# A decoder layer's kernel: the head norm's root argument on other engines, a bank kept free, the latent in another tile, and a rewritten end

## Chip, core and metric

The kernel runs on one core of one Trainium2 chip. The metric is the device time of one execution in microseconds (us); of several runs the median is given. The engines' short names are PE (TensorE, with PEld for its weight loads), DVE (VectorE), ACT (ScalarE), POOL (GpSimd) and SP (SyncE, which here only issues transfers). A `q` behind a name is the engine's instruction queue.

## The reference

Everything is float32; 4 sequences (`b`) of 512 tokens, 512 channels. Three blocks follow each other, each with a residual sum and a layer norm (mean and variance over the channels, epsilon 1e-5):

```python
x = layernorm(x + attn(x))            # differential attention
x = layernorm(x + mamba(ctx, z=x))    # convolution, selective scan, gate
x = layernorm(x + experts(x))         # shared expert + 16 routed experts

# attn: 8 heads, each of two softmax maps; 4 groups g of two heads share k and v
p   = softmax(q1 @ k1.T * s, causal) - lam * softmax(q2 @ k2.T * s, causal)
o   = p @ v                                                # [512 tokens, 256] per head
o   = o * rsqrt(mean(o*o, -1) + 1e-5) * subln_w * (1 - LAMBDA_INIT)   # the head norm
out = concat(o) @ out_w.T + out_b

# mamba: for 512 channels d and 16 states n, along the tokens
state = state * exp(dt * A) + dt * u * B;   y = sum_n(state * C) + D * u;   y * silu(z)

# experts: xl = x @ Wdown.T (the latent, 128 wide); 8 of 16 experts by sigmoid gate
shared = (x @ sw1.T * relu(x @ swg.T)**2) @ sw2.T
acc    = sum_e w[:, e] * ((xl @ rw1[e].T * relu(xl @ rwg[e].T)**2) @ rw2[e].T)
out    = shared + acc @ Wup.T
```

## The kernel before, in words

**Recording and ordering.** The body does not issue instructions directly. `nc` is a `Notes` object that records every operation as a `Step` with the tiles it reads and writes, its engine, and a sort key: `nc.key` (a due time that the code sets for each piece of work) plus an entry of the table `SHIFT`, looked up by the output's name and the engine's first letter (`"ps_y.t"` is a matmul into `ps_y`, `.v` VectorE, `.s` ScalarE or SyncE, `.g` GpSimd). `Notes.order` then runs through the steps with a table of durations (`cost`), gives each idle engine the ready step with the lowest key, and keeps tile buffers and PSUM banks within their counts. The result is one fixed instruction order for each engine; an engine runs its own queue strictly in that order. All instructions are issued from one line, L360 (L358 for pairs of small matmuls), so the profile is read by tile names rather than lines.

**Attention.** 16 units (group `g` outside, sequence `b` inside), two heads (`hh`) each. `project_T` makes `kT` and `qT`, matmuls into `ps_v` make the values `v`, which DVE adds a bias to. For each of four query tiles `i`, `softmax` makes scores `s` and probabilities `e` with row sums `l1`, `l2`. The first map is left undivided by its row sum `l1` (the head norm takes the factor out again), so the norm's epsilon is multiplied with `l1` squared. `values` transposes `e` into `pt`, copies it to `pT`, multiplies with `v` into `po`, copies that to `o`, and squares it on ScalarE with the sum in `ms` (`sq`). After the fourth tile, DVE forms `rs = EPS * l1 * l1` and `ms = ms/256 + rs`, GpSimd raises `ms` to the power -1/2 (`rs`), ScalarE scales the four tiles of `o` by `rs`, TensorE transposes them (`pt_o`), ScalarE evicts them as `oT`, and the output projection `ps_out` is added to `res`. `pt`, `pt_o` and the other transposes share one PSUM bank.

**Scan.** For each sequence 16 states by two channel halves: DVE multiplies (`h<-du,bc`), scans (`TENSOR_TENSOR_SCAN`), multiplies again (`h<-h,bc`), and GpSimd issues the transfer that adds `h` into the DRAM tensor `y` (`y<-h`). These run all along attention and the first experts, beside TensorE's work.

**Experts.** For each sequence: gate the scan's output, transpose, norm, gate matmuls `ps_gate` (16 router columns and the latent). ScalarE copies the latent by tokens to `xr`, TensorE transposes it into `xl`. The shared expert makes `sh`. For 16 experts by two halves `k`: `pg` and `ph` matmuls, `glu` (ScalarE: relu, square; DVE: `ht`), and a matmul into `pa`, which gathers all 32 parts. `pa` of the first sequence lies in the general pool `mm` (three PSUM banks, shared with `ph`, `ps_out`, `ps_qk`, `ps_y` and others), later ones in the bank that `po` leaves. At the end `pa` is copied to `aT`, and four output tiles `ps_y` sum `aT @ w_u` and two products of `sh` with `w_s2`. DVE adds each to `res`; the last sequence's tiles are normed and stored one by one by `layernorm` (DVE: statistics, aggregate, epsilon; GpSimd: power; DVE: `nb = -mean*rs`; ScalarE: scale and shift).

**Start.** Eight matmuls of the identity (`warm`) run while the first inputs are loaded. Then come `ps_in` (the scan's input projection) and the first unit's `ps_qk`. GpSimd adds the output bias (`obb`) to the four `res` tiles early on, 4.5 us each.

Of the kernel before, what the change touches and what calls it, by code (L numbers as in the profile page):

```python
# [13 lines left out]
AF = mybir.ActivationFunctionType  # L14
# [6 lines left out]
ENGINES = ("tensor", "vector", "scalar", "gpsimd", "sync")  # L21

SHIFT = {
    "aT.s": 19.9, "a_neg.s": 36.7, "a_neg.v": -21.7, "bc.s": 12.7, "bq.s": -11, "bvb.s": 13.2, "cT.s": -0.7,
    "cb.s": -0.3, "cf.v": 2.5, "cw.s": -33.1, "da.g": -5.7, "da.s": -3.1, "db.s": 9.1, "dsk.s": -4, "dt.s": -3.6,
    "dt.v": 19.7, "du.s": 2.1, "du.v": 45.5, "e.s": 10.2, "e.v": -5.1, "gb.s": 3.8, "h.v": -4.8, "ht.v": -0.6,
    "kT.s": 17.3, "l.v": 4.6, "ln_mv.v": 1.1, "ln_nb.v": -14, "ln_rs.g": 3.8, "ln_st.v": 13, "ln_ve.v": -5.5,
    "lo.v": 6.9, "lp.v": 40.1, "ls.s": 2.8, "ls.v": -10.5, "lt.s": 3.2, "m.v": 10.9, "ms.v": -5.6, "nlam.v": -5.1,
    "o.s": -40.2, "oT.s": 3.2, "obb.s": 21.3, "ow.s": 7.5, "pT.s": 3.5, "pa.t": 1.2, "pg.t": 2.7, "pg_s.t": -3.5,
    "ph.t": 2.9, "ph_s.t": 8.6, "po.t": -3.4, "pr.s": -22.7, "pr.v": -34.8, "ps_dt.t": -22.1, "ps_gate.t": -14.1,  # L30
    "ps_in.t": -19, "ps_out.t": 5.2, "ps_qk.t": 1.6, "ps_v.t": 7.7, "ps_x.t": -7, "ps_y.t": 10.3, "pt_l.t": -7.1,
    "pt_o.t": 3.5, "pt_w.t": 2.9, "pt_x.t": -4.1, "pt_y.t": -4.7, "qT.s": 2.2, "relu.s": 2.4, "relu_s.s": -25.5,
    "res.g": -40.7, "res.s": 16, "res.v": -6.4, "rp.v": -25.4, "rs.g": 0.6, "rs.v": -5.3, "s.t": 0.9, "sc.v": 9.1,
    "sg.s": -0.9, "sg.v": 2.6, "sgc.s": 1.1, "sh.v": 6, "sp.v": 12.9, "sq.s": 7.2, "sub.s": -33, "sub.v": -20.3,
    "v.v": -7.9, "w.s": -14.5, "wT.s": -0.7, "w_dg.s": -3.6, "w_dt.s": 61.7, "w_e.s": 28.1, "w_in.s": -28,
    "w_s.s": -13.3, "w_u.s": 11, "w_xp.s": 5.5, "warm.t": 30.4, "wb.s": 2.9, "wk.s": -12.1, "wq.s": 7.5, "wv.s":
    7.6, "x2T.s": 1.4, "xT.s": 1.8, "xd.s": 27.7, "xl.s": 1.6, "xm.g": 17.6, "xm.s": 2.9, "xr.s": -4.7, "xw.v":
    6.5, "y.g": -9.3, "y.s": 6.5, "y.v": -44.5, "yb.s": 7.2, "yb.v": 0.4,
}
B, S, HID = 4, 512, 512  # L40
NT = S // P
# [7 lines left out]
C2 = 6  # L49
# [109 lines left out]
def cost(engine, name, out, ins, kw):  # L159

    n = columns(out) if isinstance(out, View) else 0
    psum = any(isinstance(v, View) and v.buf.pool.psum for v in ins)
    if engine == "tensor":
        if name == "pair":
            return 0.15 + n * 0.00168, 0.35, 0.0
        if name == "transpose":
            return 0.11 * max(1, n / 128), 0.35, 0.0
        return max(n * 0.00168, 0.13), 0.35, 0.0
    if name == "dma_start":
        size = max(v.shape[0] * columns(v) * 4 if isinstance(v, View) else 0 for v in (out, *ins))  # L170
        add = kw.get("accum_op") is not None
        return {"sync": 0.45, "gpsimd": 0.95, "scalar": 0.1}[engine], 4.2 if add else 2.3, size / 230e3 * (1 + add)
    if engine == "gpsimd":
        if any(v is ALU.pow for v in ins):
            return 1.3, 0.5, 0.0
        return 0.15 + 0.0026 * n, 0.5, 0.0
    if engine == "scalar":
        wide = isinstance(kw.get("scale"), View) or isinstance(kw.get("bias"), View)
        return (
            0.19 + 0.00079 * n + (0.1 if wide else 0.0) + (0.15 if kw.get("accum_out") is not None else 0.0), 0.3, 0.0  # L180
        )
    if name == "tensor_tensor_scan":
        return 0.05 + 0.00223 * n, 0.25, 0.0
    if name in ("tensor_reduce", "bn_stats"):
        n = columns(ins[0])
    if n <= 8:
        return 0.2, 0.25, 0.0
    if name == "scalar_tensor_tensor":
        return 0.12 + 0.00125 * n, 0.25, 0.0
    if name == "tensor_scalar" and not psum:  # L190
        return 0.1 + (0.00085 if any(isinstance(v, View) for v in ins[1:]) else 0.00058) * n, 0.25, 0.0
    return 0.13 + (0.00108 if psum else 0.0011) * n + (0.1 if name == "tensor_tensor_reduce" else 0.0), 0.25, 0.0


class Notes:
# [54 lines left out]
    def order(self, keys, window=100.0):  # L250
# [24 lines left out]
        while events:  # L275
# [11 lines left out]
            for e in ENGINES:  # L287
# [4 lines left out]
                for s in ready[e]:  # L292
                    if ready_at[s.at] > now or keys[s.at] > most:
                        continue
                    if s.name == "dma_start" and landed[e][-8] > now:
                        continue

                    if s.shares and port > now:
                        continue
                    rank = (keys[s.at] + (10.0 if s.table not in (None, table) else 0.0), s.at)  # L300
                    if best is not None and rank >= least:
                        continue

                    if all(
                        b in live
                        or free[b.pool, b.tag] >= (2 if s.name == "pair" and b.pool.psum else 1)
                        and (b.pool.psum or b in due[b.pool, b.counts[-1]][: free[b.pool, b.counts[-1]]])
                        for b in s.bufs
                    ):
                        best, least = s, rank  # L310
# [63 lines left out]
def decoder_kernel(  # L374
# [33 lines left out]
    def small(shape, tag, bufs=8):  # L408
        return sb.tile(shape, tag, tag, bufs)
# [120 lines left out]

    nc.key = -60.0
    pw = ps.tile([P, S], "tr", "warm", 1)
    for i in range(8):
        nc.tensor.matmul(pw[:, :P], lhsT=ident, rhs=ident, start=True, stop=True)


# [33 lines left out]
    def values(e, v, i, o, ms):  # L570
        w = (i + 1) * P
        pt = ps.tile([P, S], "tr", "pt", 1)
        for j in range(i + 1):
            nc.tensor.transpose(pt[:, j * P : (j + 1) * P], e[:, 0, j * P : (j + 1) * P], ident)
        pT = sb.tile([P, S], "pT", "pT", 2)
        nc.scalar.copy(pT[:, :w], pt[:, :w])
        po = ps.tile([P, 256], "po", "po", 1)
        for j in range(i + 1):
            nc.tensor.matmul(po, lhsT=pT[:, j * P : (j + 1) * P], rhs=v[:, j, :], start=(j == 0), stop=(j == i))
        nc.scalar.copy(o[:, i, :], po)  # L580
        sq = sb.tile([P, 256], "sq", "sq", 1)
        nc.scalar.activation(sq, po, AF.Square, accum_out=ms[:, i : i + 1])

    def attention(n):

# [25 lines left out]
        for hh in range(2):  # L611
# [12 lines left out]
                values(e, v, i, o, ms)  # L624

            rs = small([P, NT], "rs", 4)
            nc.vector.scalar_tensor_tensor(rs, l1, EPS, l1, ALU.mult, ALU.mult)
            nc.vector.scalar_tensor_tensor(ms, ms, 1.0 / 256, rs, ALU.mult, ALU.add)
            nc.gpsimd.tensor_tensor(rs, ms, mhalf, ALU.pow)
            for i in range(NT):  # L630
                nc.scalar.activation(o[:, i, :], o[:, i, :], AF.Copy, scale=rs[:, i : i + 1])
# [126 lines left out]
    nc.sync.dma_start(out=w_s[:, 0, :, :], in_=swgT.rearrange("(c p) n -> p c n", p=P))  # L758
    nc.sync.dma_start(out=w_s[:, 1, :, :], in_=sw1T.rearrange("(c p) n -> p c n", p=P))
    w_s2 = load([P, 2, HID], sw2T.rearrange("(c p) n -> p c n", p=P), "wq", "w_s2", 2)  # L760
    w_u = load([P, HID], wuT, "wq", "w_u", 2)

    def glu(pg, ph, dst, r):
        nc.scalar.activation(r, pg, AF.Relu)
# [3 lines left out]
    def experts(b):  # L768
# [26 lines left out]


        nc.key += 10.0
        pls, xr = [], sb.tile([P, NT, LAT], "c2", "xr", C2, 1)
        for k in range(2):
            pl = ps.tile([P, 2, 256], "mm", "ps_gate", 3)  # L800
            for i in range(2):
# [57 lines left out]
        for e in range(NE):  # L859
# [10 lines left out]
            for k in range(2):  # L870
                nc.key = t_expert(b, e + 0.5 * k)
                pg = ps.tile([P, S], "s", "pg", 3)
                nc.tensor.matmul(pg, lhsT=w_e[:, 0, k * P : (k + 1) * P], rhs=xl, start=True, stop=True)
                ph = ps.tile([P, S], "mm", "ph", 3)
                nc.tensor.matmul(ph, lhsT=w_e[:, 1, k * P : (k + 1) * P], rhs=xw, start=True, stop=True)
                ht = sb.tile([P, S], "c2", "ht", C2, 2)
                glu(pg, ph, ht, sb.tile([P, S], "e", "relu", 3, 2))
                nc.key += DOWN
                nc.tensor.matmul(
                    pa, lhsT=w_e[:, 2, k * LAT : (k + 1) * LAT], rhs=ht,  # L880
                    start=(e == 0 and k == 0), stop=(e == NE - 1 and k == 1),
                )
# [1 line left out]
        aT = sb.tile([P, S], "pT", "aT", 2)  # L884
        nc.scalar.copy(aT, pa)
        for i in range(NT):
            po = ps.tile([P, HID], "mm", "ps_y", 3)
            nc.tensor.matmul(po, lhsT=aT[:, i * P : (i + 1) * P], rhs=w_u, start=True, stop=False)
            for k in range(2):
                nc.tensor.matmul(  # L890
                    po, lhsT=sh[:, k, i * P : (i + 1) * P], rhs=w_s2[:, k, :], start=False, stop=(k == 1)
                )
            nc.vector.tensor_tensor(res[b][:, i, :], res[b][:, i, :], po, ALU.add)
            if b == B - 1:
                layernorm(res[b], res[b], (i,))
                nc.sync.dma_start(out=out[b, i * P : (i + 1) * P, :], in_=res[b][:, i, :])
        if b < B - 1:
            layernorm(res[b], res[b])
# [68 lines left out]
```

## Time and profile before

| | |
|---|---|
| median of 5 runs | 1527.24 us (1526.95 to 1529.09) |
| the profiled execution | 1526.95 us, its span 1525.2 us |
| instructions | 15976 |
| granted TensorE clock | 1.00 |
| busy: PE, DVE, ACT, POOL | 99%, 78%, 63%, 13% |

The span runs from the first to the last instruction of the program. A fp32 matmul stands in the profile as two records (two passes); with 512 columns each shows some 0.593 us, but the next one starts 0.429 us later, as they are pipelined: a PE that starts a record every 0.429 us is at its pace, and "busy" covers a little of what comes after. A wait is named by what ended it. In the busy table by stretches, each engine has its busy time and, in brackets, its number of instructions; in a chain, each row is start, duration and what ran.

### The profile page before, as it was taken

The numbers are of one execution on the slowest core, as the hardware profiler recorded it, in microseconds if no ns is written. First come the engines' busy times: TensorE is split into PE (matmuls) and PEld (weight loads), VectorE is DVE, ScalarE is ACT, GpSimd is POOL, SyncE is SP. The second block draws the span as 40 slices with busy tenths as digits, with TensorE's granted clock in tenths as the row PEclk, the third lists the DMA queues.
The fourth block names the chain that finished last, engine by engine and source line by source line (L and its number), as shares of the span: only waits on it lengthen the run. The fifth ranks groups of instructions, "written<-read, shape, count | busy, mean of one in ns | idle before, by whom it ended". The sixth has DMA issues, their size and how long they took to land.

```text
span 1525.2 us, 15976 instructions
## 1 busy us (share of the span) xinstructions
PE 1512.4 (99%) x5008; PEld 845.9 (55%) x5008; DVE 1196.3 (78%) x2036; ACT 956.6 (63%) x2130; POOL 203.6 (13%) x208
## 2 busy tenths in 40 slices
PE   9999999999999999999999999999999999999997
PEld 5566565555656656565665656655445444445443
DVE  5479899798998989998898998999889953543433
ACT  3785666668666566876556678677866553444443
POOL 4111111110211110122111111111111100000000
PEclk9999999999999999999999999999999999999999
DMA  8136686554668764466864565556866842442341
GB/s 272 57 88 107 138 188 132 98 112 97 106 132 187 131 143 71 107 131 130 180 127 113 106 116 138 126 128 133 202 156 156 220 125 70 152 126 68 109 130 39
DMA packets 105749, 196.23 MB, mean 129 GB/s; under 512 B 10977, under 2 KB 46049, under 8 KB 105665
## 3 DMA queue, kind: packets, MB, share of 16 engines
q1 hardware_dynamic: 86944, 127.57, 29.8%
q0 software_dynamic: 18432, 67.12, 25.9%
q8 instruction: 40, 0.66, 0.2%
q10 hardware_dynamic: 288, 0.52, 0.1%
q14 instruction: 45, 0.36, 0.1%
HBM read 119.28 MB, written 75.89 MB: 128 GB/s over the span
## 4 chain that ended last, share of the span: by engine, by line
PE 97%; DVE 2%; ACT 1%; issue 0%; POOL 0%; POOLq 0%; DVEq 0%
PE ps_qk L360 21%; PE ps_out L360 14%; PE s L360 9%; PE po L360 9%; PE ph L360 7%; PE ps_v L360 7%; PE pa L360 7%; PE pg L360 7%; PE ps_y L360 3%; PE pt L360 2%; PE pt_o L360 2%; PE ph_s L360 2%; PE pg_s L360 2%; PE ps_in L360 2%; PE ps_gate L360 1%; PE ps_dt L358 1%
## 5 line engine op out<-in xcount | busy, mean ns | idle before, releaser
L360 DVE TENSOR_TENSOR_SCAN h<-da,h 128x1024 f32<-128x1024 f32 x128 | 292.9, 2288 | 3.1
L360 PE MATMUL ps_qk<-xT,wq 128*128 128x512 f32 x512 | 240.8, 594 | 0.0
L360 PE MATMUL ps_out<-ow,oT 128*128 128x512 f32 x512 | 236.2, 593 | 0.0
L360 POOL DMA_DIRECT2D y<-h x128 | 111.1, 868 | 788.9 <-DVE h L360 657.4
L360 ACT ACTIVATE da<-dt,a_neg 128x512 f32<-128x512 f32 (+1 forms) x256 | 175.1, 716 | 36.1 <-DVE h L360 35.9
L360 DVE TENSOR_TENSOR ht<-relu,ph 128x512 f32<-128x512 f32 x128 | 87.6, 685 | 132.9 <-ACT relu L360 103.3
L360 ACT ACTIVATE relu<-pg 128x512 f32<-128x512 f32 x128 | 76.0, 593 | 152.9 <-PE pg L360 124.5
L360 PE MATMUL s<-kT,qT 128*128 128x384 f32 (+3 forms) x512 | 164.0, 435 | 0.0
L360 ACT ACTIVATE e<-e,nm 128x256 f32<-128x256 f32 (+3 forms) x256 | 141.6, 556 | 32.3 <-DVE nm L360 31.6
L360 PE MATMUL po<-v,pT 128*128 128x256 f32 x640 | 159.4, 380 | 0.4 <-ACT pT L360 0.4
L360 DVE CUSTOM_DVE_ANT_0 e<-s,mask 128x256 f32<-128x256 f32 (+3 forms) x256 | 119.8, 487 | 49.0 <-PE s L360 42.3
L360 DVE TENSOR_TENSOR h<-h,bc 128x1024 f32<-128x1024 f32 x128 | 156.3, 1221 | 1.2
L360 DVE TENSOR_TENSOR h<-du,bc 128x1024 f32<-128x1024 f32 x128 | 156.0, 1219 | 0.1
L360 PEld LDWEIGHTS po<-v,pT 128*128 128x128 f32 x640 | 121.4, 190 | 60.5 <-issue 37.4
L360 PEld LDWEIGHTS ps_out<-ow,oT 128*128 128x128 f32 x512 | 93.4, 191 | 87.6 <-issue 82.8
L360 PEld LDWEIGHTS ps_qk<-xT,wq 128*128 128x128 f32 x512 | 92.7, 191 | 77.3 <-issue 70.9
L360 PE MATMUL pa<-ht,w_e 128*128 128x512 f32 x256 | 131.0, 594 | 0.6 <-DVE ht L360 0.6
L360 PE MATMUL ph<-xw,w_e 128*128 128x512 f32 x256 | 130.5, 593 | 0.2 <-DVE xw L360 0.2
L360 PE MATMUL pg<-xl,w_e 128*128 128x512 f32 x256 | 129.5, 593 | 0.0
L360 PE MATMUL ps_qk<-xT,wk 128*128 128x512 f32 x256 | 121.0, 594 | 0.0
L360 PE MATMUL ps_v<-wv,xT 128*128 128x256 f32 x512 | 119.0, 380 | 1.3 <-DVE v L360 1.3
L360 PEld LDWEIGHTS s<-kT,qT 128*128 128x128 f32 x512 | 87.6, 191 | 55.2 <-issue 44.0
(123 smaller groups left out, 2006.0 us busy)
## 6 DMA issues: line engine op xcount, KB each, us to landing
y<-h POOLq DMA_DIRECT2D x128, 512.0 KB, 7.9
bc<-bc SPq DMA_DIRECT2D x64, 512.0 KB, 6.4
wb<-w SPq DMA_DIRECT2D x64, 256.0 KB, 3.6
xT<-in_xT_dram SPq DMA_DIRECT2D x15, 1024.0 KB, 7.6
w_e<-in_rwgT_dram SPq DMA_DIRECT2D x64, 128.0 KB, 2.2
w_e<-in_rw1T_dram SPq DMA_DIRECT2D x64, 128.0 KB, 2.3
w_e<-in_rw2T_dram SPq DMA_DIRECT2D x64, 128.0 KB, 2.5
wq<-in_wqkvT_dram SPq DMA_DIRECT2D x8, 512.0 KB, 8.1
```

Of the source, the lines that this page charges most:

```text
L358: self.nc.tensor.matmul(out, lhsT=lhsT, rhs=rhs, **{"start": True, "stop": True, **s.kw})
L360: getattr(getattr(self.nc, s.engine), s.name)(*[get(a) for a in s.args], **{k: get(v) for k, v in s.kw.items()})
```

## The change

- The head norm: the sum of squares is scaled by 1/256 at its source (scale 1/16 inside ScalarE's square), `rs = EPS * l1 * l1` becomes a square on ScalarE, and the sum `ms + rs` an addition on GpSimd, ahead of the power there. Both DVE instructions go.
- Banks: `ph` of the first sequence gets a name of its own with at most 2 of the 3 `mm` banks, `ps_y` at most 2. The planner's condition for taking a bank now looks at all counts of a tile.
- The latent by tokens `xr` lies in the second half of a tile whose first half is `w_u`, no longer in a buffer of the pool `c2`.
- The ends: 5 warm-up matmuls for 8; each `ps_y` sums the `sh` products first and `aT @ w_u` last; the last output tile is computed in two halves of 256 columns; the last sequence's norm is written out, with the scaling in one DVE instruction in place of `nb` and ScalarE's activation.
- A small GpSimd step is costed at 1.0 by the planner (0.15 before), and `SHIFT` has new numbers throughout, so every engine's order is new.

```diff
 SHIFT = {
...
-    "kT.s": 17.3, "l.v": 4.6, ... "ls.s": 2.8, "ls.v": -10.5, ... "nlam.v": -5.1,
+    "kT.s": 20.3, "l.v": 4.9, ... "ls.s": 37.6, "ls.v": -18.2, ... "nlam.v": -8.4,
-    ... "ps_y.t": 10.3, ... "res.g": -40.7, "res.v": -6.4, ... "rs.g": 0.6, ... "v.v": -7.9,
+    ... "ps_y.t": 19.9, ... "res.g": -51.3, "res.v": -25.2, ... "rs.g": -8, ... "v.v": -0.6,
...
@@ cost
-        return 0.15 + 0.0026 * n, 0.5, 0.0
+        return (1.0 if n <= 8 else 0.15 + 0.0026 * n), 0.5, 0.0
@@ Notes.order
-                        or free[b.pool, b.tag] >= (2 if s.name == "pair" and b.pool.psum else 1)
+                        or min(free[b.pool, c] for c in b.counts) >= (2 if s.name == "pair" and b.pool.psum else 1)
@@ warm
-    for i in range(8):
+    for i in range(5):
@@ values
-        nc.scalar.activation(sq, po, AF.Square, accum_out=ms[:, i : i + 1])
+        nc.scalar.activation(sq, po, AF.Square, scale=1.0 / 16, accum_out=ms[:, i : i + 1])
@@ attention
-            nc.vector.scalar_tensor_tensor(rs, l1, EPS, l1, ALU.mult, ALU.mult)
-            nc.vector.scalar_tensor_tensor(ms, ms, 1.0 / 256, rs, ALU.mult, ALU.add)
+            nc.scalar.activation(rs, l1, AF.Square, scale=math.sqrt(EPS))
+            nc.gpsimd.tensor_tensor(ms, ms, rs, ALU.add)
             nc.gpsimd.tensor_tensor(rs, ms, mhalf, ALU.pow)
@@ weights of the experts
-    w_u = load([P, HID], wuT, "wq", "w_u", 2)
+    w_ux = sb.tile([P, 2, HID], "wq", "w_u", 2)
+    w_u = w_ux[:, 0, :]
+    nc.sync.dma_start(out=w_u, in_=wuT)
@@ experts
-        pls, xr = [], sb.tile([P, NT, LAT], "c2", "xr", C2, 1)
+        pls, xr = [], w_ux[:, 1, :].split(NT)
...
-                ph = ps.tile([P, S], "mm", "ph", 3)
+                ph = ps.tile([P, S], "mm", "ph" if b else "ph0", 3, 0 if b else 2)
...
         for i in range(NT):
-            po = ps.tile([P, HID], "mm", "ps_y", 3)
-            nc.tensor.matmul(po, lhsT=aT[:, i * P : (i + 1) * P], rhs=w_u, start=True, stop=False)
-            for k in range(2):
-                nc.tensor.matmul(
-                    po, lhsT=sh[:, k, i * P : (i + 1) * P], rhs=w_s2[:, k, :], start=False, stop=(k == 1)
-                )
-            nc.vector.tensor_tensor(res[b][:, i, :], res[b][:, i, :], po, ALU.add)
-            if b == B - 1:
-                layernorm(res[b], res[b], (i,))
+            parts = 2 if (b, i) == (B - 1, NT - 1) else 1
+            n = HID // parts
+            st = small([P, 2, 6], "ln_st", 2)
+            for p in range(parts):
+                at = slice(p * n, (p + 1) * n)
+                po = ps.tile([P, n], "mm", "ps_y", 3, 2)
+                for k in range(2):
+                    nc.tensor.matmul(
+                        po, lhsT=sh[:, k, i * P : (i + 1) * P], rhs=w_s2[:, k, at], start=(k == 0), stop=False
+                    )
+                nc.tensor.matmul(po, lhsT=aT[:, i * P : (i + 1) * P], rhs=w_u[:, at], start=False, stop=True)
+                nc.vector.tensor_tensor(res[b][:, i, at], res[b][:, i, at], po, ALU.add)
+                if b == B - 1:
+                    nc.vector.bn_stats(out=st[:, p, :], in_=res[b][:, i, at])
+            if b == B - 1:
+                mv = small([P, 2], "ln_mv", 2)
+                rs = small([P, 1], "ln_rs", 2)
+                nc.vector.bn_aggr(out=mv, in_=st[:, :parts, :])
+                nc.vector.tensor_scalar(rs, mv[:, 1:2], EPS, None, ALU.add)
+                nc.gpsimd.tensor_tensor(rs, rs, mhalf[:, 0:1], ALU.pow)
+                nc.vector.tensor_scalar(
+                    res[b][:, i, :], res[b][:, i, :], mv[:, 0:1], rs, ALU.subtract, ALU.mult
+                )
                 nc.sync.dma_start(out=out[b, i * P : (i + 1) * P, :], in_=res[b][:, i, :])
```

More of the change, by code (lines that the diff above doesn't have):

```diff
@@ L23 @@
 SHIFT = {
[L24 to L38, printed above, removed]
+    "aT.s": 15.1, "a_neg.s": 29.2, "a_neg.v": -26.8, "bc.s": 4.2, "bq.s": -10.4, "bvb.s": 1.3, "cT.s": 2.7,
@@ new lines @@
+    "cb.s": -10.4, "cf.v": 7.6, "cw.s": -27.6, "da.g": -25.4, "da.s": -3.2, "db.s": 3.7, "dsk.s": -5, "dt.s":
+    -2.6, "dt.v": 18.3, "du.s": -1.9, "du.v": 48.9, "e.s": 10.1, "e.v": -6.1, "gb.s": 2.1, "h.v": -10.2, "ht.v":
+    -9.6, "kT.s": 20.3, "l.v": 4.9, "ln_mv.v": 0.4, "ln_nb.v": 7.9, "ln_rs.g": 5.6, "ln_rs.v": 1.3, "ln_st.v":
+    11.1, "ln_ve.v": -18.4, "lo.v": 14.3, "lp.v": 27.5, "ls.s": 37.6, "ls.v": -18.2, "lt.s": 8.2, "m.v": -1.8,
+    "ms.g": 0.5, "nlam.v": -8.4, "o.s": -53.4, "oT.s": -10.1, "obb.s": 17.3, "ow.s": 16.2, "pT.s": 5.7, "pa.t": 1,
@@ new lines @@
+    "pg.t": 0.8, "pg_s.t": 1.5, "ph.t": -8, "ph_s.t": 9, "po.t": -3.4, "pr.s": -22, "pr.v": -34.2, "ps_dt.t":
+    -23.5, "ps_gate.t": -8.1, "ps_in.t": -19.8, "ps_out.t": 5.9, "ps_qk.t": 2.8, "ps_v.t": 6.8, "ps_x.t": -3.6,
+    "ps_y.t": 19.9, "pt.t": -0.7, "pt_l.t": -5.7, "pt_o.t": 2.3, "pt_w.t": -2.9, "pt_x.t": -11.9, "pt_y.t": -6.9,
+    "qT.s": 8.1, "relu.s": 6.7, "relu_s.s": -17.3, "res.g": -51.3, "res.s": 15.5, "res.v": -25.2, "rp.v": -29,
+    "rs.g": -8, "s.t": 1.8, "sc.v": 9.2, "sg.s": 1.7, "sg.v": 2.1, "sgc.s": 3.7, "sh.v": 12.5, "sp.v": 13.8,
@@ L39 @@
+    "sq.s": 6, "sub.s": -36, "sub.v": -6.3, "v.v": -0.6, "w.s": -8.1, "wT.s": 2.9, "w_dg.s": -6.2, "w_dt.s": 74.4,
+    "w_e.s": 17.9, "w_in.s": -35.6, "w_s.s": -18, "w_u.s": 13.4, "w_xp.s": 18.5, "warm.t": 24.2, "wb.s": -6.2,
+    "wk.s": -17.7, "wq.s": 26, "wv.s": 19.8, "x2T.s": -2.6, "xT.s": -9.6, "xd.s": 13.4, "xl.s": 6.5, "xm.g": -1.4,
+    "xm.s": -4.1, "xw.v": 7.1, "y.g": -30.3, "y.s": 6, "y.v": -46.5, "yb.s": -3.2, "yb.v": -3.8,
 }
```

## The prediction

> **What bounds the kernel now.** I first read the page: TensorE (PE) is busy 1512.4 of 1525.2 us, VectorE (DVE) 78%, ScalarE (ACT) 63%, GpSimd (POOL) 13%. A pipelined PE can look busy without being full, so next I read the busy time by stretches, with edges at the ends of the start-up, of the first attention work, of attention, of the hand-over to the experts, and of the expert loop:
>
> ```profile
> core 0: us, PE busy (x) PEld busy (x) DVE busy (x) ACT busy (x) POOL busy (x), PEclk, DMA share, GB/s
> 0.00:5.10 5.10, 3.34 (x16) 3.35 (x17) 0.00 (x0) 1.28 (x1) 1.69 (x16) 1.00 0.66 206
> 5.10:33.00 27.90, 26.62 (x82) 12.70 (x81) 20.27 (x22) 13.08 (x19) 9.43 (x4) 1.00 1.00 328
> 33.00:1000.00 967.00, 967.00 (x3445) 580.32 (x3446) 840.65 (x1444) 654.97 (x1605) 153.37 (x150) 1.00 0.59 122
> 1000.00:1100.00 100.00, 98.20 (x341) 53.74 (x340) 91.99 (x162) 75.54 (x161) 17.59 (x15) 1.00 0.67 153
> 1100.00:1500.00 400.00, 399.77 (x1089) 188.68 (x1088) 234.21 (x388) 205.16 (x337) 19.30 (x20) 1.00 0.47 129
> 1500.00:1525.20 25.20, 17.52 (x40) 7.07 (x38) 9.20 (x23) 6.54 (x10) 2.18 (x4) 0.97 0.11 42
> ```
>
> PE's idle time is 1.76 + 1.28 + 0 + 1.80 + 0.23 + 7.68 = 12.75 us: nothing for 967 us of attention, and over half of it in the last 25 us. In the timeline a 512-column matmul record starts every 0.429 us (three expert matmuls, six records, every 2.57 us), so a full PE is really at its pace. No edit takes matmuls away except the warm-up. What can be won is therefore the idle time, and the chain behind the last matmul. The waits of PE name the first:
>
> ```profile
> PE warm L360 <- POOL ident masks.py:199: 1.8, 1, 1.8
> PE ps_v L360 <- DVE v L360: 1.3, 1, 1.3
> PE pt_o L360 <- ACT oT L360: 1.0, 1, 1.0
> PE ps_y L360 <- ACT aT L360: 0.7, 1, 0.7
> PE pa L360 <- DVE ht L360: 0.6, 2, 0.4
> PE po L360 <- ACT pT L360: 0.4, 1, 0.4
> PE ph L360 <- DVE xw L360: 0.2, 1, 0.2
> ```
>
> A wait costs a little more than is shown, as a matmul's modelled end covers part of it. By starts against the 0.429 us pace (0.109 for a transpose) the timeline gives 1.44 at 31.3 (`ps_v`), 0.57 and 1.14 at 1014 to 1017 (`po`, `pt_o`), 0.33 at 1058.5 (`ph`), 1.12 at 1091 to 1093 (`pt_o` behind `o`), 0.40 at 1224 (`pa`): 5.0 us ahead of the end. The chain of waits gives the end:
>
> ```profile
> 1505.43 0.70 DVE ht L360
> ...
> 1506.18 1.14 PE pa L360 x2
> 1507.34 0.59 ACT aT L360
> 1507.98 10.58 PE ps_y L360 x24
> 1518.58 0.70 DVE res L360
> 1519.31 0.70 DVE ln_st L360
> 1521.12 0.17 DVE ln_nb L360
> 1521.32 0.81 ACT res L360
> ```
>
> PE stands still for `ht` and `aT`, then 24 records run, then one tile's norm runs alone. The last store is issued at 1522.16 and lands at 1524.16.
>
> **The end.** Today the first `ps_y` matmul needs `aT`. After the change the two products with `sh`, ready long before, come first. From the last but one `pa` pair (start 1504.80) to the first `ps_y` record (1507.98) is 3.18 us for four records of 0.429 = 1.72 us: 1.46 us lost. Two output tiles may hold banks, so four `sh` products (3.4 us) are there to fill it; I take 1.4. The two-bank limit should not stop PE: tile 2 needs tile 0's bank, whose addition ends some 0.95 us after its last matmul, while PE has 1.7 us of tile 1 to do.
>
> Behind the last matmul: today from 1518.58 to 1522.13 is 3.55 us, of which 3.23 is work (0.69 + 0.69 + 0.18 + 0.15 + 0.55 + 0.16 + 0.81). After it only the last half's addition (0.42, the row of `v` from PSUM at 256 columns), its statistics (between 0.18, the aggregate's row, and 0.69; I take 0.40, a little over half), the aggregate 0.18, the epsilon 0.15, the power 0.55, and the normalization on DVE. That last is not in the trace: half of the 1024-column TENSOR_SCALAR with fixed scalars (0.687) is 0.34, the 512-column SCALAR_TENSOR_TENSOR is 0.75; I take 0.50, nearer the first as it too reads one tile. Sum 2.20, and 0.27 between instructions: 2.47, so 1.1 us less (0.8 to 1.4). Against it: DVE now also normalizes, 2.2 us a tile, and tiles 0 and 1 finish 0.86 us apart. Ahead of the last half's addition stand 3 x 2.21 + 0.82 = 7.45 us of DVE work in the 6.85 us that PE leaves; 0.1 to 0.6 us late, I take 0.4. The twelve half records of 0.216 cost what six of 0.429 do. End: 1.4 + 1.1 - 0.4 = **2.1 us gained** (1.0 to 2.7).
>
> **The root's argument.** It removes 64 short DVE instructions (0.155 + 0.154 us, 32 times: 9.9 us), adds 32 ACT squares of four columns (between 0.187, the row of `ls` at two columns, and 0.39, the 256-column square: 6 to 12 us) and 32 additions on POOL. The square reads `l1`, complete some 10 us before the sums; ACT at 63% takes it in its gaps, and 0.3 us where it has none. The scale on `sq` is free. The addition stands in POOL's queue ahead of the power, so behind every `y` accumulation there, as the power is now. What POOL takes is in the answer on `rs`:
>
> ```profile
> L360 POOL TENSOR_TENSOR rs<-ms,mhalf x32: 1027/1886/3316, 67.1 to 1087.8; 128x4 f32<-128x4 f32 x32
> ```
>
> In the timeline 16 values are 1.03; 9 are 1.9 to 2.4, each beside one of DVE's `h` multiplications (1.22), and 7 are 2.9 to 3.3, each beside a scan (2.29): POOL waits out DVE's long two-input instructions. I bound the addition by 0.54 (the one-column power) and 3.3 and take 1.0, the power's undisturbed value. DVE's step falls out of the chain, 0.16 and its place in DVE's queue: from the last sum to the power's start 0.3 to 2.3 us pass today, typically 1.1. So a head's chain grows by about nothing to 1 us. Between the end of its first scaled `o` and the first `pt_o` transpose the timeline shows 0.05 to 8.9 us; under 1.1 us seven times (0.36, 1.02, 0.65, 1.02, 0.55, 1.08, and 0.05 for the last head). The new costs of the planner (1.0 for a small POOL step) let it put `pt_o` later; for the last head, where PE already waits 1.12 us, I count +0.9.
>
> [...]
>
> **Banks, latent, order.** `ph` of the first batch limited to two banks: `pa` holds the third for most of that batch anyhow; nothing. `ps_y` limited to two: the expert loop hides it (0.23 us idle in 400). The latent in half of `w_u`'s tile frees one of six `c2` buffers; same copy, no new transfer. The condition for banks and the new shifts rewrite all orders, so the 5.0 us ahead of the end are dealt anew. 1.44 us of them come from DVE's `nlam`, which took 4.5 us while POOL added `obb` beside it; with `ls` 35 later in its key that meeting may be gone. The others hang on single evictions. I take half of them back, 2.5 us; bounds +5.0 and, for fresh stalls as large as the old, -5.0.
>
> **Warm-up.** Three matmuls fewer end it 1.05 us earlier, at about 4.05, but the first inputs land at 4.51, against 5.11 for the first `ps_in` today: at best 0.5 us. The granted clock rises at 4.86 today. With PE idle from 4.05 to 4.5 it may rise later; each us of half clock costs 0.5 us. What is lost or won up to 1.4 us is taken up by the `ps_v` wait at 31.3 if that stays: I take 0.
>
> [...]
>
> **Sum.** 2.1 + 2.5 - 0.9 = 3.7 us off the profiled run's 1526.95 (its span 1525.2 and 1.75 around it): 1523.25. The median of the runs is 0.29 above that run: **1523.5**.
>
> **Rivals.**
> *Only the end gains (0.27).* The new order stalls as much as the old, the POOL step is covered: 1527.24 - 2.1 = 1525.1. For it: the middle already has PE idle for 3.3 us in 1495. Against: 1.44 us have a named cause that the keys move.
> *GpSimd's queue sets the heads (0.18).* The addition too meets an `h` multiplication and costs 1.9: the seven tight heads expose (1.9 less each cover) 1.54 + 0.88 + 1.25 + 0.88 + 1.35 + 0.82 + 1.85 = 8.6 us, and 1527.24 - 2.1 + 8.6 = 1533.7. Slower than today from 2.1 us exposed on, measurably from 5.1 on. For it: 16 of 32 powers took 1.9 us or more. Against: DVE's queue wait goes, and other matmuls can be put ahead of `pt_o`.
> *The end's gain is eaten by DVE.* If DVE's backlog is 1 us longer, 1524.5; inside the forecast's own range.
>
> **How the numbers follow.** The forecast has 0.55, its own range 1520.8 to 1525.0. About 0.2% or 3 us is what a measurement here can tell from no change, so faster means below 1524.2: 0.50 of the forecast and 0.03 of the first rival; slower means above 1530.3: 0.15 of the second; the rest 0.32. The range goes from 1520.3 (end at 2.7, nearly all middle stalls gone) to 1530.0, where two thirds of the second rival and a little at the bottom are left out.
>
> **What would show it.** Right: `sh` products standing before the last `aT`, no wait of `ps_y` for it, PE's idle time after 1500 at 6 us or less; the last chain 2.3 to 2.7 us; POOL 32 instructions more at 1.0 to 1.9 us; no `ps_v` wait near 31. Wrong: new waits of `pt_o` for `o` at several heads (second rival), a slow clock past 6 us, PE idle over 2 us between 1000 and 1100, or the last half's addition waiting behind other DVE work for over 1 us.

## The result, and the profile after

The changed kernel takes 1533.43 us in the median of 26 runs (1527.96 to 1537.78), the kernel before 1527.68 us in 47 runs beside it (1526.37 to 1529.73): 1.003 times as long in the mean, 95% interval 1.0022 to 1.0037. It is slower, by 0.3%, where the forecast was 1523.5 us. The times of the changed kernel fall into two groups with nothing between: 11 at 1528.0 to 1528.8, 15 at 1533.1 to 1537.8. The profiled run (1533.50 us, span 1531.7) is of the upper one, so the first question is what makes that group.

The busy time by stretches, with the edges of before:

```profile
0.00:5.10 5.10, 2.85 (x11) 2.55 (x12) 0.00 (x0) 1.28 (x1) 1.69 (x16) 1.00 0.65 197
5.10:33.00 27.90, 24.21 (x60) 10.57 (x59) 20.53 (x20) 14.80 (x19) 9.33 (x3) 1.00 0.68 221
33.00:1000.00 967.00, 965.63 (x3430) 576.97 (x3431) 836.31 (x1375) 654.83 (x1623) 168.12 (x179) 1.00 0.59 124
1000.00:1100.00 100.00, 97.48 (x350) 55.52 (x349) 93.02 (x166) 74.89 (x163) 16.04 (x18) 1.00 0.64 143
1100.00:1500.00 400.00, 400.00 (x1097) 189.48 (x1097) 234.36 (x388) 206.22 (x343) 19.26 (x20) 1.00 0.49 133
1500.00:1531.70 31.70, 25.38 (x66) 12.07 (x64) 13.02 (x29) 7.94 (x13) 2.35 (x4) 0.94 0.13 45
```

PE idles 2.25 + 3.69 + 1.37 + 2.52 + 0 + 6.32 us. The second row tells most: PE has 60 records in it where it had 82. The waits of PE, longest first:

```profile
PE ps_x L358 <- DVE y L360: 3.0, 1, 3.0
PE warm L360 <- POOL ident masks.py:199: 1.8, 1, 1.8
PE po L360 <- ACT pT L360: 1.0, 3, 0.5
PE ph L360 <- DVE ht L360: 0.9, 1, 0.9
PE ps_qk L360 <- DVE v L360: 0.8, 1, 0.8
```

Idle time misses a PE that works at half clock (below: a record every 0.853 us in place of 0.429). So I also count its lag: the time at which a record starts, less the work of all records started before it at the pace (0.429 us for 512 columns, and so on; the warm-up matmuls are not counted as work). The lag only grows; where it grows, time is lost.

| lag of PE, us | at 20 | at 40 | at 100 | at 1000 | at 1100 | at 1500 | last record |
|---|---|---|---|---|---|---|---|
| before | 5.1 | 7.3 | 8.6 | 13.0 | 16.8 | 17.9 | 19.5 |
| after, profiled run | 7.1 | 13.5 | 15.1 | 21.5 | 25.9 | 26.2 | 26.2 |
| after, a run of the lower group (`e5_same`) | 5.8 | 6.6 | 8.8 | 15.3 | 19.7 | 19.9 | 19.9 |

The upper group's loss is made in the first 40 us: 13.5 against 7.3. Behind that both groups go alike. The timeline shows the start (start us, duration us, engine, work, idle before it):

```profile
4.76 9.35 PE L360 MATMUL ps_in<-cT,w_in 128*128 128x512 f32 x16 [0.50 <-DMA cT<-in_ctxT_dram]
...
22.79 9.23 POOL L360 TENSOR_TENSOR res<-res,obb 128x2048 f32<-128x2048 f32 x2 [8.01 <-DMA res<-in_x_dram]
...
23.25 4.33 DVE L360 TENSOR_TENSOR nlam<-ls 128x1 f32<-128x1 f32 x1
...
28.04 5.07 DVE L360 TENSOR_TENSOR y<-y,sgc 128x1024 f32<-128x1024 f32 x1
...
33.16 1.95 PE L358 MATMUL ps_x<-y,w_xp 128*48 128x256 f32 x8 [3.00 <-DVE y L360]
```

The same stretch of the kernel before, where both `y*sgc` run ahead of the additions:

```profile
5.11 7.03 PE L360 MATMUL ps_in<-cT,w_in 128*128 128x512 f32 x16
...
21.60 1.23 DVE L360 TENSOR_TENSOR y<-y,sgc 128x1024 f32<-128x1024 f32 x1
...
23.41 8.98 POOL L360 TENSOR_TENSOR res<-res,obb 128x2048 f32<-128x2048 f32 x2 [9.93 <-DMA obb<-in_ob_dram]
...
27.89 4.51 DVE L360 TENSOR_TENSOR nlam<-ls 128x1 f32<-128x1 f32 x1
...
33.00 2.00 PE L360 MATMUL ps_v<-wv,xT 128*128 128x256 f32 x8 [1.28 <-DVE v L360]
```

The 16 `ps_in` records, 7.03 us before, take 9.35: the granted clock rises at 9.24 us, not 4.86. (The trace's record of the clock begins at these times, and `PEclk` counts what lies ahead as 1.00; there the pace shows it, a `ps_in` record every 0.853 us up to 9.19 us, every 0.429 from 9.65 on.) Everything that hangs on them comes later, and `nlam`, one element in each partition, is issued 0.46 us after GpSimd has begun its first bias addition. It lasts 4.33 us, until that addition is over; `y*sgc` behind it falls into the second addition and lasts 5.07. PE waits 3.0 us for it, and then the clock falls once more:

```profile
33.20:36.50 3.30, 3.30 (x10) 1.46 (x11) 0.01 (x1) 0.36 (x1) 0.00 (x0) 0.50 0.05 12
```

In a trace of the lower group (`e5_same`) the clock rose at 6.89 us; `nlam` goes ahead of the addition, and only `y*sgc` is held, for 2.2 us, nearly all of which PE has other work for:

```profile
21.99 0.16 DVE L360 TENSOR_TENSOR nlam<-ls 128x1 f32<-128x1 f32 x1
...
22.16 9.98 POOL L360 TENSOR_TENSOR res<-res,obb 128x2048 f32<-128x2048 f32 x2 [8.64 <-DMA res<-in_x_dram]
...
24.36 3.40 DVE L360 TENSOR_TENSOR y<-y,sgc 128x1024 f32<-128x1024 f32 x1 [1.67 <-ACT sgc L360]
```

Here `nlam` starts 0.17 us ahead of the addition, in the profiled run 0.46 us behind it: that is all that stands between the two cases. The rows show the size of the hold: in the profiled run `nlam`, which came second, lasts until 27.58 us, the addition until 27.56; in the kernel before `nlam` lasts until 32.40 us, the second addition until 32.39.

### The profile page after: what moved, and what is told of

It reads as the page before. It is cut to its first block, busy times and chain, and to the rows that moved or that the text cites. A ratio compares the mean times of both kernels' runs of the same rounds, so it can differ in the third digit from the quotient of the medians.

```text
span 1531.7 us, 15956 instructions
## 1 busy us (share of the span) xinstructions
PE 1515.6 (99%) x5008; PEld 847.2 (55%) x5008; DVE 1197.2 (78%) x1974; ACT 960.0 (63%) x2160; POOL 216.8 (14%) x240
## 4 chain that ended last, share of the span: by engine, by line
PE 96%; DVE 2%; DMA 1%; POOL 1%; ACT 1%; issue 0%; POOLq 0%; SPq 0%; ACTq 0%
PE ps_qk L360 21%; PE ps_out L360 14%; PE po L360 9%; PE s L360 8%; PE pa L360 7%; PE ps_v L360 7%; PE ph L360 7%; PE pg L360 7%; PE ps_y L360 3%; PE pt L360 2%; PE ps_in L360 2%; PE pg_s L360 2%; PE ph_s L360 2%; PE pt_o L360 2%; PE ps_gate L360 1%; PE ps_x L358 1%
## 5 line engine op out<-in xcount | busy, mean ns | idle before, releaser
L360 ACT ACTIVATE e<-e,nm 128x128 f32<-128x128 f32 (+3 forms) x256 | 142.0, 557 | 27.8 <-DVE nm L360 26.7
L360 DVE CUSTOM_DVE_ANT_0 e<-s,mask 128x128 f32<-128x128 f32 (+3 forms) x256 | 120.3, 487 | 43.6 <-PE s L360 41.2
L360 PE MATMUL ps_v<-wv,xT 128*128 128x256 f32 x512 | 115.9, 379 | 0.0
L360 PEld LDWEIGHTS s<-kT,qT 128*128 128x128 f32 x512 | 84.5, 191 | 45.8 <-issue 34.8
```

The lines of the kernel that those rows point to most:

```text
L360: getattr(getattr(self.nc, s.engine), s.name)(*[get(a) for a in s.args], **{k: get(v) for k, v in s.kw.items()})
```

## The experiments

Theory 1: in the start the bias additions on GpSimd hold VectorE, and TensorE waits (1a: which of `nlam` and the first addition comes first decides the group). Theory 2: the cut warm-up and the late clock alone. Theory 3: the new order in the middle, or the root's addition on GpSimd. Unless said otherwise, a kernel keeps the instruction order of its parent on every engine; the edits are made where `Notes.trace` issues the ordered steps (`for s in done`). "Upper" counts the runs over 1530.5 us; kernels of a set share the chip. The kernel before has upper runs too, 3 of 171 over all sets (1532.2, 1536.6 and 1536.7 us). Of all upper runs only two were traced, the profiled one above and that of `e9_w0`; a rarer second cause is not excluded.

**First set.** Before: 1527.52 us.

`e1_w8`, three more warm-up matmuls in the changed kernel:

```diff
+            if s.name == "matmul" and s.bufs[0].name == "warm":
+                for _ in range(MORE.pop() if MORE else 0):   # MORE = [3]
+                    self.nc.tensor.matmul(...)                # the same warm-up matmul
```

> The changed kernel with eight warm-up matmuls as before and every queue's order as after the change. Theory 1 (the bias additions on GpSimd hold VectorE's two-input instructions in the first 35 us, and TensorE waits for those): the clock rises near 4.9 us again and TensorE is 2 us ahead at 20 us, but the wait of ps_x for y at 33 us takes it back; the time stays at that of the changed kernel within 1 us (1532 to 1535). Theory 2 (the cut warm-up and the late clock are the whole loss): 1526 to 1528 and no spread between runs. Theory 3 (the new order in the middle, or the root's addition on GpSimd): as the changed kernel.

1528.31 us, 4 of 12 upper (1532.0 to 1532.7). The group does not go with the warm-up back: theory 2 falls as the whole cause. Theory 1 expected the loss in every run, whatever the clock; a third of the runs have it. The traced run is a lower one, with the clock up at 5.87.

`e2_noadd`, the bias additions left out:

```diff
+            if s.engine == "gpsimd" and s.name == "tensor_tensor" and columns(s.args[0]) == NT * HID:
+                continue
```

> The changed kernel without the four additions of the output bias to the residual on GpSimd (the output lacks this bias); all else and all orders as they are. Theory 1: nlam and y*sgc take their own 0.2 and 1.2 us instead of 4.3 and 5.1, the ps_x wait of 3.0 us and the second fall of the clock go; 1527 to 1529.5, the late clock's 2 us remaining. Theory 2: stays at 1532 to 1535. Theory 3: stays there too, or within 1 us of it.

1525.84 us, 1525.25 to 1526.46, none upper, although the clock in its trace rose only at 7.70. `nlam` takes 0.158 us. Better than theory 1 said, by 1.2 us: by the medians the additions cost the lower group 2 us as well (1527.85 in `e5_same`, of the second set).

`e3_b_w5`, the kernel before with five warm-up matmuls:

```diff
+                MORE.append(1)                                # in the same place, MORE = []
+                if len(MORE) > 5:
+                    continue
```

> The kernel before with five warm-up matmuls in place of eight, every order as it was. Theory 1: the clock rises only at some 8 to 9 us, TensorE loses 2 us by 20 us, and the ps_v wait at 31 us (1.4 us) takes most of it: 1527.5 to 1529. Theory 2: 1532 to 1535. Theory 3: as the kernel before.

1527.17 us, none of 11 upper; 0.999 times the kernel before, interval 0.9978 to 1.0002. The cut warm-up alone costs the old order nothing that shows in the times. How a late clock is made up for there is not shown: in the trace (1527.90 us, the second slowest) the clock rose at 5.77, not at 8 to 9, and the `ps_v` wait did not shrink, as theory 1 has it, but grew from 1.3 to 2.0 us.

`e4_dveroot`, the root's argument on VectorE again, in the changed order:

```diff
-  scalar.activation(rs, l1, AF.Square, scale=math.sqrt(EPS));  gpsimd.tensor_tensor(ms, ms, rs, ALU.add)
+  vector.scalar_tensor_tensor(rs, l1, EPS, l1, ALU.mult, ALU.mult)
+  vector.scalar_tensor_tensor(ms, ms, 1.0, rs, ALU.mult, ALU.add)
```

> The changed kernel with the root's argument formed by two VectorE instructions again, put where GpSimd's addition stood, all other orders as they are. Theory 3 (the addition on GpSimd lengthens the heads' chains): 2 us or more faster than the changed kernel. Theories 1 and 2: within 1 us of it, since in the changed kernel's profile pt_o waits for o only 0.6 us in all.

1527.87 us, 2 of 12 upper; the ten others 1527.76, against 1527.85 for the lower group of `e5_same`. From 40 to 1100 us its lag grows by 12.5, that of `e5_same` by 13.1: 0.6 us at most.

**Second set.** Before: 1527.44 us.

`e5_same`, the changed kernel again:

> The changed kernel once more, beside the others of this set. Two groups of times are expected, near 1528 and at 1533 to 1538. Theory 1a (a race in the start: nlam on VectorE is issued a moment before or after GpSimd's first bias addition, and if after, it and y*sgc are each held for one addition): the groups differ in nothing but the first 40 us. Theory 3 (middle order): the groups would differ later too.

1528.02 us, 2 of 11 upper (1533.24, 1534.13). The share of the upper group, and with it the median, differs from set to set: 15 of 26, 2 of 11, 3 of 11 (`e15_same`). The changed kernel is slower in each: 1.003, 1.0011 and 1.0017 times the kernel before, no interval reaching 1.

`e6_split`, each addition in four:

```diff
+                for i in range(NT):                           # in place of one 128x2048 addition
+                    self.nc.gpsimd.tensor_tensor(get(r[:, i, :]), get(r[:, i, :]), o[:, i, :], ALU.add)
```

> The changed kernel with each bias addition on GpSimd cut into its four token tiles (16 additions of about 1.15 us for 4 of 4.5), orders as they are. Theory 1a: a held VectorE instruction waits 1.2 us at most, the upper group goes; 1526.5 to 1528, all in one group. If what counts is GpSimd's total time on these additions (18 us) and not the length of one: as the changed kernel, with two groups.

1526.69 us, 1525.57 to 1527.63, none upper. In this trace the clock rises late, at 8.44, and `nlam` comes 0.25 us after the start of the first addition, as in the upper group; but now:

```profile
22.53 8.42 POOL L358 TENSOR_TENSOR res<-res,obb 128x512 f32<-128x512 f32 x6 [8.22 <-DMA res<-in_x_dram]
...
22.78 1.07 DVE L365 TENSOR_TENSOR nlam<-ls 128x1 f32<-128x1 f32 x1
...
25.15 2.23 DVE L365 TENSOR_TENSOR y<-y,sgc 128x1024 f32<-128x1024 f32 x1 [0.76 <-ACT sgc L365]
```

GpSimd's total is no less (16 additions of 1.26 us for 4 of 4.5), so what makes the upper group is the length of one addition.

`e7_b_end`, the kernel before with the new end, for the last sequence only (the loop over `i` of the diff above, under `b == B - 1`); the other orders stay until the last 25 us:

> The kernel before with the new end of the last sequence alone (sh products first, last tile in halves, its norm on VectorE); every queue as before until the last 25 us. The prediction's end term: 2.1 us faster than the kernel before (1.0 to 2.7). Rival, that the store's landing hides the norm's chain: 1.4 us or less.

1525.42 us: 2.0 us less than the kernel before (by the ratio, 0.9987, interval 0.9971 to 1.0002, one run of 11 at 1534.74 included). The interval just takes in 1; the median agrees with the end term of the sum.

`e8_b_noadd`, the kernel before without the additions (the edit of `e2_noadd`):

> The kernel before without the four bias additions on GpSimd (the output lacks this bias). Theory 1a: the ps_v wait of 1.3 us goes, a_neg and nlam take 0.2 us each; 1 to 1.5 us faster than the kernel before, and 0 to 1 us faster than the changed kernel without them (1525.84), as the new order loses in the middle what the end gains. If the additions harm only the new order: no gain here.

1524.82 us, 2.6 less, twice what was expected. Two stalls of the kernel before are missing in its trace: the `ps_v` wait (1.44 us by starts), which is the additions' doing, and the 1.12 us at 1091 to 1093 us (`pt_o` behind `o`). The second lies a thousand us behind the last addition, and why it went is not shown. It beats the changed kernel without them by 1.0 us, although only the latter has the new end.

**Third set.** Before: 1527.65 us.

`e9_w0`, the changed kernel with no warm-up matmul (every `warm` step skipped):

> The changed kernel without any warm-up matmul, orders as they are: the granted clock should rise late (after 8 us) in every run. If a late clock is what throws the start into the upper group (the work on y comes 1.5 us later, so nlam is issued after GpSimd's first bias addition has begun): all or nearly all runs at 1532 to 1538, nlam over 3 us in the trace. If the group is decided by something else (landing of the loads, say): two groups as before, moved by 1 us at most.

1534.67 us, all of 6 upper (one at 1530.99). The clock rises at 10.73, `nlam` starts at 27.93 under the second addition and lasts 4.45 us, and `ps_qk` waits 4.9 us for the `v` eviction behind it. It comes so late because the last multiply-add ahead of it (`y<-xm,cw,y`) was held by the first addition, until 27.46. So a start with no warm-up makes the upper group in every run, in this trace by the same hold but not by the same instructions.

`e10_w8_split` was meant to have eight warm-up matmuls and the additions in parts; its trace shows 4.5 us additions, so it lacks the parts and only repeats `e1_w8`.

> The changed kernel with eight warm-up matmuls and the bias additions in four parts each. With the race gone the warm-up is worth what the clock alone costs: 0.3 to 1.5 us faster than with five and parts (1526.69): 1525.2 to 1526.4. If warm-up matmuls count for nothing then: 1526.7.

1528.25 us, 1 of 11 upper. With `e1_w8`: 5 of 23, where five warm-up matmuls have 20 of 48; too few runs to say that the share differs.

`e11_oldshift`, the changed code with parts, ordered by the old shift numbers:

```diff
-SHIFT = { ... after ... }
+SHIFT = { ... before ... }
```

> The changed code with the old shift numbers (so other orders everywhere), bias additions in parts, against the changed kernel with parts (1526.69). If the new numbers are what costs the middle (3 us more of stalls between 100 and 1100 us than the kernel before): 1524 to 1526. If it is the changed steps themselves (root on GpSimd, bank limits, planner's cost): 1526.5 to 1529.

1528.77 us, slower than with the new numbers (1526.69). From 100 to 1000 us its lag grows by 5.0, before by 4.4, after by 6.4, and from 100 to 1100 us by some 3 us less than in `e6_split`, which differs from it in the numbers alone: there the new numbers are what costs. But between 1200 and 1300 it grows by 4.4, where the others lose 0.1 to 0.9. Each order has stalls of its own, and the old numbers with the changed steps come out no better. (The traced run, 1530.02 us, is the slowest of the eleven.)

`e12_best`, the new end and the additions in parts on the kernel before:

> The kernel before with the new end for the last sequence and the bias additions in parts, all other orders as before. The end alone gave 2.0 us less, leaving the additions out 2.6; with parts a held instruction waits 1.2 us at most: 1523 to 1524.5, faster than both kernels. If parts give nothing here: 1525.4.

1525.32 us, 0.9986 of the kernel before (0.9978 to 0.9995), so faster than both kernels; but not beyond `e7_b_end`. With 1.26 us `nlam` no longer makes PE wait for `v`, yet most of what leaving the additions out gave is not had; the stall ahead of `pt_o` is still there, at 1092 us.

**Fourth set.** Before: 1527.34 us.

`e13_nlam_late`, one swap on VectorE's queue of the changed kernel, full-length additions:

```diff
-  nlam, nlam, v<-ps_v,bvb, y<-y,sgc, a_neg
+  v<-ps_v,bvb, y<-y,sgc, nlam, nlam, a_neg
```

> The changed kernel with one swap on VectorE's queue: nlam's two instructions after the first eviction of v and the second y*sgc instead of ahead of them; all other queues and the 4.5 us bias additions as they are. Theory 1a (nlam's place makes the upper group: held itself, it holds y*sgc back into the next addition): y*sgc meets one addition at most, ps_x waits under 1 us, one group at 1526.5 to 1528.5. If the additions hold whatever stands there: two groups as in the changed kernel.

1528.45 us, 1 of 11 upper (`e15_same`: 3 of 11), which by the counts alone could be chance. The trace says more, for it has the upper group's case: the clock rises at 9.66, and the addition starts (23.05) before `ls` is ready for `nlam` (23.47).

```profile
23.05 10.24 POOL L365 TENSOR_TENSOR res<-res,obb 128x2048 f32<-128x2048 f32 x2 [8.01 <-DMA res<-in_x_dram]
...
25.88 3.04 DVE L365 TENSOR_TENSOR y<-y,sgc 128x1024 f32<-128x1024 f32 x1 [2.09 <-ACT sgc L365]
...
28.84 4.47 DVE L365 TENSOR_TENSOR nlam<-ls 128x1 f32<-128x1 f32 x1
...
29.24 1.07 PE L363 MATMUL ps_x<-y,w_xp 128*48 128x256 f32 x8
```

`ps_x` does not wait, the clock does not fall again, the lag at 40 us is 8.0 against 13.5, and the span 1527.2 against 1531.7 us, although `nlam` is still held for 4.5 us. What made the one upper run was not profiled.

`e14_w8_parts`, eight warm-up matmuls and the parts together:

> The changed kernel with eight warm-up matmuls and the bias additions in four parts each (checked to hold both). With the race gone the warm-up is worth what the clock alone costs: 0.3 to 1.5 us less than with five and parts (1526.69): 1525.2 to 1526.4. If the warm-up counts for nothing then: 1526.5 to 1527.

1526.41 us, 1526.06 to 1527.31; 0.93 below the kernel before of its set, where `e6_split` is 0.75 below that of its own. The warm-up is worth 0.2 us, which these runs can't tell from nothing.

`e15_same`, the control:

> The changed kernel on this chip, as control: two groups, 1527 to 1529 and 1533 to 1538, with between two of eleven and six of eleven runs in the upper one.

1528.51 us, 3 of 11 upper.

## Why the prediction was wrong

**The start: the step that failed.** "What is lost or won up to 1.4 us is taken up by the `ps_v` wait at 31.3 if that stays: I take 0." It did not stay, and the late clock cost more than 1.4: 2.0 us by 20 us in the profiled run, where the clock rose 4.4 us later. Nor is it shown that the wait absorbs such a loss even in the old order (`e3_b_w5`). In the new order the lateness decides besides whether `nlam` is issued before or after GpSimd's addition (23.25 us here, 21.99 in the lower group's trace); that is worth some 4 us more: the rest of the 6.2 between 13.5 and 7.3. The prediction saw the 4.5 us `nlam`, named GpSimd as its cause, saw that the key of its input `ls` moved by 35, and drew only "that meeting may be gone". The new order did not take `nlam` out of the additions' way; it put it at the edge of the first, ahead of `y*sgc`, which PE needs. That the price of a collision depends on what is queued behind the held instruction was not asked. The prediction's own sign for it, a slow clock past 6 us, came true (9.24).

**The middle: wrong in sign.** I took half of 5.0 us back. From 100 to 1500 us the lag grows by 11.1 after (26.2 - 15.1) and by 9.3 before (17.9 - 8.6): 1.8 us lost, not 2.5 won, and its sign of being wrong came true as well: PE idles 2.52 us between 1000 and 1100 us. The new waits are the same kind as the old, evictions a little late (`po` for `pT` 1.0 us, `ph` for `ht` 0.9). A new order deals such waits anew, and "half of them back" had no row behind it. Which edit or key makes each was not tried one by one, so the cause of each stays open: `e4_dveroot` rules out the root's engine, and `e11_oldshift` shows that the new numbers cost some 3 us up to 1100 us and that the old ones, with the changed steps, lose it elsewhere. This step fails the forecast without any collision too. In the lower group's trace the start to 40 us is even 0.7 us better than before, but from 40 to 1500 us the lag grows by 13.3 against 10.6, and with the end's gain the kernel is no faster: 1528.02 us in the median of `e5_same`.

**The end: right, as far as the runs can tell.** 2.1 us forecast, 2.0 measured (`e7_b_end`, and 2.3 with the parts in `e12_best`). In the changed kernel's trace PE's fill gave 1.57 (1.4 forecast) and the chain behind it 0.3 (3.55 before, 3.24 now; 0.7 forecast). The chain of the changed kernel:

```profile
1516.79 8.61 PE ps_y L360 x26
1525.40 0.02 issue
1525.42 0.42 DVE res L360
1525.84 0.10 DVE ln_mv L360
1525.95 0.02 issue
1525.97 0.15 DVE ln_rs L360
1526.12 0.67 DVE ln_st L360 x2
1526.79 0.02 issue
1526.82 0.22 DVE ln_mv L360
1527.04 0.02 issue
1527.06 0.16 DVE ln_rs L360
1527.22 0.02 issue
1527.25 0.02 POOLq L360
1527.27 0.07 issue
1527.33 0.75 POOLq L981
1528.08 0.03 issue
1528.11 0.55 DVE res L360
```

From the last addition to the end of the norm is 3.24 us, where 2.47 and 0.4 of backlog were forecast. The last half's addition came in time; DVE's backlog came behind it: tile 2's aggregate and epsilon, and both halves' statistics; and the last power took 0.71 in place of 0.54, beside tile 2's normalization. A normalization took 0.54 (0.50 forecast).

**The root's argument: mechanism right, price too high.**

```profile
L360 POOL TENSOR_TENSOR ms<-ms,rs x32: 193/396/2230, 68.8 to 1096.3; 128x4 f32<-128x4 f32 x32
L360 POOL TENSOR_TENSOR rs<-ms,mhalf x32: 1017/1038/3100, 69.1 to 1097.4; 128x4 f32<-128x4 f32 x32
```

The addition takes 0.19 us undisturbed and 0.40 in the median; I took 1.0, the power's row, which is nearest in shape but not in work. Beside a scan on DVE (2.29 us) it is up to 2.2. The scale on `sq` showed no cost: 0.390 us in the median in both traces. The power behind the addition fell from 1.89 to 1.04 in the median: the addition now meets part of those instructions in its place. (With the root's argument on VectorE, `e4_dveroot`, it is 1.36, so part of the fall is the new order's.) `pt_o` waited for `o` 0.2 us in all: the new order gives the heads room, and 0.9 us became 0 within 0.6 (`e4_dveroot`). The second rival, heads set by GpSimd's queue, is wrong though its sign came true and its 1533.7 us lies 0.3 from the median: that is luck, for the engine was right, the place was not, and the median depends on how many runs are upper ones.

**Sum for the profiled runs** (1533.50 less 1526.95 = 6.55): start to 40 us 6.2, 40 to 100 us 0.3, 100 to 1500 us 1.8, PE's end -1.6, the rest -0.15.

## What to carry to other kernels

When GpSimd runs a long two-input elementwise instruction (4.5 us here), list the VectorE instructions that can come due beside it, and for each what is queued behind it: one element per partition was held as long as a tile (`nlam` 4.33 us for 0.16, `y*sgc` 5.07 for 1.22). Cut such GpSimd instructions into parts (1.26 us each in `e6_split`: no run upper), or put what TensorE waits for ahead. A change that shifts the start by a microsecond has to be costed at both sides of every near race; a time that falls into two groups can be a sign of one, and the first row of the lag where the groups part shows where. Don't credit a rewritten order with the stalls of the old one.

## What the runs showed of the hardware

- The clock's rise varies from run to run: 9.24 us in the profiled run, 6.89 in `e5_same`, the same kernel. The number of warm-up matmuls did not set it alone: with eight it came at 4.86 in the kernel before and at 7.14 in `e8_b_noadd`, with five at 5.77 in `e3_b_w5` and at 9.66 in `e13_nlam_late`, with none at 10.73 in `e9_w0`. The second stretch at half clock lasted 3.41 us, from 33.14 to 36.55, behind a wait of 3.0 us; that of `e9_w0`, with its wait of 4.9 us, 6.83 us.
- VectorE's held instructions ended within 0.1 us of the end of a GpSimd addition, or ran their own length after it (`y*sgc` in the profiled run: until 33.11 us, 1.09 after the second addition's end at 32.02; 1.22 undisturbed, at 19.73). `a_neg`, which reads one tensor from SBUF and a fixed scalar, was held as well (3.21 us in the kernel before, 0.18 free); the second `nlam` instruction, of the same form but one element wide, was not (0.15 us under the second addition, at 27.61 in the profiled run).
